# Attention gated by an FFN: the output projection in float16 pairs, and the heads of two query blocks in alternation

## Chip, cores and metric

The kernel runs on one core of a Trainium2 chip. The metric is device time in microseconds (us) of one execution; lower is better.

## What is computed

The input x is 1024 rows of 512. With xn its layer norm, the result is x + s · silu(f), where s is the attention of xn and f a gated feed-forward network of xn with weights kept as integers, scales and zeros in groups of 128. The reference, cut to the attention:

```python
q = (x @ Wq.T).reshape(b, s, H, HD).transpose(0, 2, 1, 3)      # 32 heads of 128
k = (x @ Wk.T).reshape(b, s, HKV, HD).transpose(0, 2, 1, 3)    # 8 groups
v = (x @ Wv.T).reshape(b, s, HKV, HD).transpose(0, 2, 1, 3)
q = _rmsnorm(q, q_norm_w)
k = _rmsnorm(k, k_norm_w)
scores = jnp.einsum('bkgqd,bksd->bkgqs', qg, k) / math.sqrt(HD)
bias = jnp.where(rel > 0, NEG_INF, slopes[:, :, None, None] * rel)   # causal, ALiBi
attn = jax.nn.softmax(scores + bias[None], axis=-1)
out = jnp.einsum('bkgqs,bksd->bkgqd', attn, v)
return out.transpose(...).reshape(b, s, H * HD) @ Wo.T
```

All of it is float32. The kernel gets that accuracy from pairs: a number is held as a high and a low part, and each product is three matmuls (`mm3`: high·high, high·low, low·high).

## The kernel before

The order of the work is written out by hand: each engine executes its instructions in the order in which the program issues them, and nothing is rescheduled. All DMAs go out from SP's queue, transposes and plain loads alike, in program order.

**The stages.** From 0 to about 137 us the program makes the gate and up products of the FFN, one of 14 column blocks at a time. From 137 to 217 us it runs the down projection: 14 passes (`it`), each with two halves (`tb`) of 12 matmuls of 512 columns. In each pass it loads, dequantizes (`dn_dequant`) and splits (`dn_split_w`, `dn_split_h`) what a later pass needs. The gate is put out to the tensor gd. Then come 12 projections (`Projection`): for each pair of key/value groups one of keys and values and two of queries, each with 8 tiles of 128 rows. Their normalized results go out to DRAM, transposed by DMA. The last projection's normalization (`inverse`, `newton`, `normalize`, `halves`) is put off and spread over steps of groups 1 to 4. During the last two projections the first eight attention steps are mixed in (`early`); the rest follow, from about 490 us to the end.

**The attention.** For each of 8 key/value groups there are 4 query blocks of 256 rows (`QB`); block qb sees 256·(qb+1) keys. A *unit* is one head of one block, and has two *steps* (`qt`), one for each 128 query rows. A step's *width* is its number of keys: 128 and 256 in block 0, 384 and 512 in block 1, 640 and 768 in block 2, 896 and 1024 in block 3. There are 256 steps, 32 in a group. Blocks come one after the other: 3, 2, 1, 0 in group 0, 2, 3, 0, 1 in groups 1 to 6, 2, 3, 1, 0 in group 7. In this text a block is eight steps.

In step n (`step`) the program issues, in this order:

- query, key and value loads that are due, and the scores of step n on TensorE (`scores`, L795 and on) into one of two PSUM buffers "s";
- the high part of a finished head (`heads_hi`, L864, ACT), which is done at step n − 10;
- for step n − 1 (`exponentials`): bias and minimum on VectorE (L816, "row"), exponential on ACT (L817);
- for step n − 3 (`split_hi`): the scaled float16 high part on ACT (L827), into one of five buffers p16;
- for step n − 4 (`split_lo`): the low part on VectorE (L836), and the DMA transpose of both parts to pT (L837);
- the low part of the finished head (`heads_lo`, L870), and the accumulation into y of a projection that is done (`accumulate`, L905 to L911);
- for step n − 9 (`AV_LAG`): the values matmuls of half the keys of that step's unit (`values`), with one projection triple (`out_proj`, three matmuls "op" of 512 columns) ahead of the last key tile.

A projection sums four heads (`part`) for each of two row tiles (`i`), so a block has eight triples. They start 18 steps after the block's first step, one a step. The head outputs oh, ol and Wo's parts woh, wol are float32r pairs. Wo is loaded and split 10 and 6 steps ahead of a group's first triple (`load_wo`; `split_wo`, with the low part on GpSimd, L782). oh carries the value scale rv of its group (L864).

In group 7 `gate_load` brings gd and x for a block, `gate_partial` on GpSimd turns y into y·gate + x, and `accumulate` multiplies the last projection by the gate, adds that and puts it out. The last block in the order has its projections (op_last) beside the heads themselves.

## Time and profile before

| What | Value |
|---|---|
| Time, median of 3 runs | 1081.96 us (1079.21 to 1083.37) |
| Profiled execution | 1087.19 us |
| Its span, first to last instruction | 1085.4 us |
| Mean granted TensorE clock | 0.987 |
| Stretch of groups 1 to 6 (steps 32 to 223) | 545.7 to 985.3 us |
| Group 7 and the end | 985.3 to 1085.4 us |

The profile is of one execution, some us from the median. Engines: PE is TensorE, PEld its weight loads (beside matmuls), DVE is VectorE, ACT is ScalarE, POOL is GpSimd, SP issues the DMAs. A line such as L836 is a line of the kernel before. A matmul's recorded duration includes its way through the array, so matmuls overlap in the record: what one costs in a full stream is the distance from start to start, and a busy PE need not be a full one. In the lists of waits the columns are the time in all, the number of waits and the longest. In the tables of stretches, each engine has its busy us and its number of instructions; then come the granted clock, the share of time that the DMA engines were busy, and GB/s. The DMA share reaches 1.20 in one stretch, so packets' times overlap in it, and a share of 1.0 is no proof of a full bandwidth.

### The profile page before, as it was taken

The page shows a single profiled execution, that of the slowest core. Times are in us where ns is not written, and L with a number is a line of the kernel's source. Part 1 is how long each engine was busy: PE and PEld are TensorE (multiplying, and loading weights), DVE is VectorE, ACT ScalarE, POOL GpSimd, SP SyncE. Part 2 cuts the span into 40 slices and gives each one's busy share as a digit, 9 for nine tenths or more (in the row PEclk, how much of TensorE's full clock was granted, in tenths as well). Part 3 has the DMA queues.
Part 4 walks back from the last instruction along what each step waited for, and adds up shares of the span by engine and source line. Part 5 has one row for each costly group of instructions (what it writes and reads, how often), then busy time and mean ns, then how long its engine had stood idle before and what let it go on. Part 6 is the DMA issues. An engine that isn't in the chain of part 4 may idle for free.

```text
span 1085.4 us, 18417 instructions
## 1 busy us (share of the span) xinstructions
PE 1025.6 (94%) x5912; PEld 621.8 (57%) x5912; DVE 885.4 (82%) x1738; ACT 797.9 (74%) x2144; POOL 362.7 (33%) x343
## 2 busy tenths in 40 slices
PE   7899899999999999997999999999899999999996
PEld 4444378744444444445667666667566676676674
DVE  7888997448777887787799897998897887979985
ACT  5777633568688776787788796887785887868872
POOL 1688653125545554341204104014031040043132
PEclk8999999999999999998999999999999999999999
DMA  5133255236989989999989999999998998999994
GB/s 198 32 114 119 67 141 155 74 124 152 237 206 202 237 196 270 223 205 203 221 170 213 190 216 193 196 201 189 206 191 178 213 201 184 193 224 220 237 192 117
DMA packets 445887, 198.10 MB, mean 183 GB/s; under 512 B 394402, under 2 KB 403934, under 8 KB 445790
## 3 DMA queue, kind: packets, MB, share of 16 engines
q1 hardware_dynamic: 445790, 196.93, 83.1%
q8 instruction: 46, 0.75, 0.3%
q14 instruction: 51, 0.42, 0.1%
HBM read 71.03 MB, written 29.36 MB: 92 GB/s over the span
## 4 chain that ended last, share of the span: by engine, by line
PE 57%; DVE 12%; ACT 11%; DMA 10%; issue 6%; POOL 2%; SPq 0%; DVEq 0%; ACTq 0%; POOLq 0%
DMA pT<-p 9%; PE gu_ps L255 6%; PE av L108 4%; PE s L108 4%; PE av L110 4%; PE av L109 4%; PE s L109 4%; PE s L110 4%; PE op L108 3%; PE op L110 3%; PE op L109 3%; ACT p L827 3%; PE ps_q L109 2%; PE ps_q L108 2%; PE ps_q L110 2%
## 5 line engine op out<-in xcount | busy, mean ns | idle before, releaser
L836 DVE SCALAR_TENSOR_TENSOR p<-pf,row,p 128x1024 f16<-128x1024 f32 (+7 forms) x256 | 216.4, 845 | 39.2 <-ACT p L827 36.3
L816 DVE CUSTOM_DVE_ANT_0 pf<-s,trel,cs 128x1024 f32<-128x1024 f32 (+7 forms) x256 | 207.5, 810 | 23.1 <-PE s L110 21.8
L817 ACT ACTIVATE pf<-pf,row 128x1024 f32<-128x1024 f32 (+7 forms) x256 | 197.0, 770 | 35.1 <-DVE row L816 33.5
L827 ACT ACTIVATE p<-pf,row 128x1024 f16<-128x1024 f32 (+7 forms) x256 | 196.9, 770 | 34.1 <-DMA pT<-p 30.1
L782 POOL TENSOR_TENSOR wol<-wor,woh 128x512 fp32r<-128x512 f32 x32 | 57.8, 1807 | 425.0 <-ACT woh L781 418.7
L108 PE MATMUL av<-pT,vT 128*128 128x256 f16 (+1 forms) x640 | 171.8, 268 | 25.6 <-DMA pT<-p 25.4
L109 PE MATMUL av<-pT,vT 128*128 128x256 f16 (+1 forms) x640 | 169.2, 264 | 0.0
L110 PE MATMUL av<-pT,vT 128*128 128x256 f16 (+1 forms) x640 | 169.2, 265 | 0.0
L108 PE MATMUL s<-kT,qT 128*128 128x512 f16 (+3 forms) x384 | 125.9, 328 | 3.8 <-DVE row L816 3.8
L109 PE MATMUL s<-kT,qT 128*128 128x512 f16 (+3 forms) x384 | 125.6, 327 | 0.0
L108 PEld LDWEIGHTS <-vT 128*128 128x128 f16 x640 | 62.5, 98 | 108.8 <-issue 84.6
L110 PE MATMUL s<-kT,qT 128*128 128x512 f16 (+3 forms) x384 | 123.8, 327 | 0.0
L108 PE MATMUL op<-woh,oh 128*128 128x512 f32 x248 | 121.9, 492 | 0.0
L864 ACT ACTIVATE oh<-av,rv 128x256 fp32r<-128x256 f32 x128 | 60.0, 468 | 57.5 <-PE av L110 56.3
L110 PE MATMUL op<-woh,ol 128*128 128x512 f32 x248 | 98.9, 399 | 0.0
L109 PE MATMUL ps_q<-wl_q,xth 128*128 128x512 f16 x256 | 97.7, 382 | 0.8 <-DVE wl_q L535 0.8
L108 PE MATMUL ps_q<-wh_q,xth 128*128 128x512 f16 x256 | 97.8, 382 | 0.6 <-ACT wh_q L534 0.6
L109 PE MATMUL op<-wol,oh 128*128 128x512 f32 x248 | 97.7, 394 | 0.0
L110 PE MATMUL ps_q<-wh_q,xtl 128*128 128x512 f16 x256 | 97.6, 381 | 0.0
L870 DVE SCALAR_TENSOR_TENSOR ol<-av,rv,oh 128x256 fp32r<-128x256 f32 x128 | 61.2, 478 | 21.8 <-ACT oh L864 21.7
L609 POOL TENSOR_TENSOR f_q<-f_q,inv_q 128x512 f32<-128x512 f32 x64 | 76.9, 1226 | 1.3
L109 PEld LDWEIGHTS <-vT 128*128 128x128 f16 x640 | 63.7, 99 | 11.9 <-issue 2.5
(184 smaller groups left out, 2263.5 us busy)
## 6 DMA issues: line engine op xcount, KB each, us to landing
qd<-tr_q SPq DMA_DIRECT2D x64, 256.0 KB, 3.5
qT<-qd SPq DMA_DIRECT2D x32, 512.0 KB, 4.4
wq<-in_wq SPq DMA_DIRECT2D x32, 256.0 KB, 4.1
wor<-in_wo SPq DMA_DIRECT2D x32, 256.0 KB, 3.6
gui<-in_gu_w SPq DMA_DIRECT2D x13, 512.0 KB, 3.6
wkv<-in_wkv SPq DMA_DIRECT2D x16, 256.0 KB, 3.8
vd<-v SPq DMA_DIRECT2D x8, 512.0 KB, 4.2
kd<-tr_kv SPq DMA_DIRECT2D x32, 128.0 KB, 2.5
```

What stands on the lines that cost most here:

```text
L108: te.matmul(ps, lhsT=lh, rhs=rh, start=first, stop=False)
L109: te.matmul(ps, lhsT=lh, rhs=rl, start=False, stop=False)
L110: te.matmul(ps, lhsT=ll, rhs=rh, start=False, stop=last)
L255: te.matmul(banks[j][:, k, :], lhsT=w[:, j, ws], rhs=x[:, j, k * 512 : k * 512 + 512], start=x is xth, stop=x is xtl)
L609: ge.tensor_tensor(f, f, ib, ALU.mult)
L782: ge.tensor_tensor(wol[g, i], raw, woh[g, i].bitcast(F32), ALU.subtract)
L816: ve.tensor_tensor_reduce(p, ps, trel[g][:, S - w :], cs[:, hh : hh + 1], 3e38, ALU.add, ALU.min, least[:, c])
L817: se.activation(p, p, AF.Exp, bias=least[:, c], scale=-1.0, accum_out=total[:, c])
L827: se.activation(p16[u, qt][:, :, 0, :], pf[u, qt], AF.Copy, scale=scale[:, qt : qt + 1])
L836: ve.scalar_tensor_tensor(lo, p, scale, hi, ALU.mult, ALU.subtract)
L864: se.activation(oh, av_ps[u], AF.Copy, scale=rv[:, g : g + 1])
L870: ve.scalar_tensor_tensor(ol, av_ps.pop(u), rv[:, g : g + 1], oh.bitcast(F32), ALU.mult, ALU.subtract)
```

## The change

**Format.** oh, ol, woh and wol become float16 instead of float32r. Wo is scaled by a factor for each group: the squares of each group's Wo rows are summed during the down projection (`wo_squares_load`, `wo_squares`: from pass 3 a load of 1 MB, two passes later a square of 128 x 2048 with a sum on ACT, eight of each), turned into an approximate reciprocal root for each group late in the projections (`wo_factors`, three short parts), and applied to each raw Wo tile on GpSimd (`scale_wo`, 8 steps ahead of the group's first triple). The value scale moves from oh into Wo, and `accumulate` undoes the factor with a scalar operand. There are four raw Wo buffers instead of two, and twelve oh and ol instead of eight.

**Order.** Groups 1 to 6 have two pairs of blocks, (2, 1) and (3, 0), of 16 steps each. Within a pair the heads alternate: head 0 of block 2, head 0 of block 1, head 1 of block 2, and so on. Groups 0 and 7 keep their order.

**Projections by step.** A table is made ahead (`op_at`, `acc_at`): a pair's 16 triples begin 10 steps after the pair's last step, one a step, so those of the first block of a pair start later than now by up to eight steps, as do all that queue behind them. For the last two blocks but the final one, two triples a step are allowed. Loads of queries, keys and values and the gate's loads and sums get steps of their own: queries at 6 and 10 of a pair, keys at 22 and values at 30 of a group, four query buffers instead of two; the last gate load at step 259 instead of 251, its sum at 263 instead of 259.

The diff, without unchanged lines and the five new small tiles:

```diff
-FIRST_ORDER = (3, 2, 1, 0)
-ORDER = (2, 3, 0, 1)
-LAST_ORDER = (2, 3, 1, 0)
+FIRST_ORDER = ((3,), (2,), (1,), (0,))
+ORDER = ((2, 1), (3, 0))
+LAST_ORDER = ((2,), (3,), (1,), (0,))
...
+KEYS_STEP = 22
+VALUES_STEP = 30
...
-KEYS_BLOCK = 2
-VALUES_BLOCK = 3
...
+WO_SCALE = 8
...
-GATE_LOADS = [25, 26, 28, 30]
-GATE_SUMS = [27, 28, 30, 31]
-GATE_STEP = 2
+GATE_LOADS = [211, 219, 235, 259]
+GATE_SUMS = [227, 243, 251, 263]
...
+OH_BUFS = 12
...
+    wo_raw = {}
+    def wo_squares_load(g):
+        wo_raw[g] = gp.tile([P, NH, DM], F32, tag=("gs", "us")[g % 2], name=f"wo_sq{g}")
+        sp.dma_start(wo_raw[g], wo[g * NH * HD : (g + 1) * NH * HD, :].rearrange("(i p) c -> p i c", p=P))
+    def wo_squares(g):
+        w = wo_raw.pop(g).rearrange("p i c -> p (i c)")
+        se.activation(w, w, AF.Square, accum_out=swo[:, g : g + 1])
...
-                ve.tensor_scalar(rv[:, 2 * self.i : 2 * self.i + 2], self.ri, 1.0 / (X_SCALE * P_SCALE), None, ALU.mult)
+                ve.tensor_scalar(rv[:, 2 * self.i : 2 * self.i + 2], self.ri, 1.0 / X_SCALE, None, ALU.mult)
...
         def split_head(self, i):
...
+                if 0 <= it - 3 < HKV:
+                    wo_squares_load(it - 3)
+                if 0 <= it - 5 < HKV:
+                    wo_squares(it - 5)
...
-    blocks = [(g, qb) for g in range(HKV) for qb in (FIRST_ORDER if g == 0 else ORDER if g < HKV - 1 else LAST_ORDER)]
-    units = [(g, qb, hh) for g, qb in blocks for hh in range(NH)]
+    blocks = [(g, qbs) for g in range(HKV) for qbs in (FIRST_ORDER if g == 0 else ORDER if g < HKV - 1 else LAST_ORDER)]
+    units = [(g, qb, hh) for g, qbs in blocks for hh in range(NH) for qb in qbs]
...
     def load_queries(g, qb):
-        qT[g, qb] = ap1.tile([P, NQT, 2, NH, P], F16, tag="qT", name=f"qT{g}_{qb}")
+        qT[g, qb] = ap1.tile([P, NQT, 2, NH, P], F16, tag="qT", name=f"qT{g}_{qb}", bufs=4)
...
+    def wo_factors(k):
+        if k == 0:
+            ve.tensor_tensor(rvs, rv, rv, ALU.mult)
+            ve.tensor_tensor(swo16, rvs, swo, ALU.mult)
+        elif k == 1:
+            wo_ps.append(ps2("wo_ps")[:, 0, :HKV])
+            te.matmul(wo_ps[0], lhsT=ones_bf, rhs=swo16, start=True, stop=True)
+        else:
+            ve.tensor_scalar(sg, wo_ps.pop(), 1.0 / W_SCALE**2, 1e-30, ALU.mult, ALU.max)
+            rsqrt_seed(sg, sg)
+            ve.reciprocal(isg, sg)
+            ve.tensor_tensor(rvs, rv, sg, ALU.mult)
     def load_wo(g, i):
-        wor[g, i] = late[0].tile([P, DM], F32, tag="wor", name=f"wor{g}_{i}", bufs=2)
+        wor[g, i] = late[0].tile([P, DM], F32, tag="wor", name=f"wor{g}_{i}", bufs=4)
...
+    def scale_wo(g, i):
+        ge.tensor_scalar(wor[g, i], wor[g, i], rvs[:, g : g + 1], None, ALU.mult)
     def split_wo(g, i):
-        woh[g, i] = late[0].tile([P, DM], F32R, tag="woh", name=f"woh{g}_{i}", bufs=5)
-        wol[g, i] = late[0].tile([P, DM], F32R, tag="wol", name=f"wol{g}_{i}", bufs=5)
+        woh[g, i] = late[0].tile([P, DM], F16, tag="woh", name=f"woh{g}_{i}", bufs=5)
+        wol[g, i] = late[0].tile([P, DM], F16, tag="wol", name=f"wol{g}_{i}", bufs=5)
...
-        ge.tensor_tensor(wol[g, i], raw, woh[g, i].bitcast(F32), ALU.subtract)
+        ge.tensor_tensor(wol[g, i], raw, woh[g, i], ALU.subtract)
...
     def relative(g):
...
     def heads_hi(u):
-        oh = late[0].tile([P, QB], F32R, tag="oh", name=f"oh{u}", bufs=8)
-        ol = late[0].tile([P, QB], F32R, tag="ol", name=f"ol{u}", bufs=8)
-        g = units[u][0]
-        se.activation(oh, av_ps[u], AF.Copy, scale=rv[:, g : g + 1])
-        oT[u] = (oh, ol)
+        oh = late[0].tile([P, QB], F16, tag="oh", name=f"oh{u}", bufs=OH_BUFS)
+        ol = late[0].tile([P, QB], F16, tag="ol", name=f"ol{u}", bufs=OH_BUFS)
+        se.activation(oh, av_ps[u], AF.Copy, scale=1.0 / P_SCALE)
+        oT[units[u]] = (oh, ol)
...
     def heads_lo(u):
-        oh, ol = oT[u]
-        g = units[u][0]
-        ve.scalar_tensor_tensor(ol, av_ps.pop(u), rv[:, g : g + 1], oh.bitcast(F32), ALU.mult, ALU.subtract)
-    nb = len(units) // NH
-    def out_proj(b, i, part):
+        oh, ol = oT[units[u]]
+        ve.scalar_tensor_tensor(ol, av_ps.pop(u), 1.0 / P_SCALE, oh, ALU.mult, ALU.subtract)
+    final = blocks[-1][0], blocks[-1][1][0]
+    def out_proj(g, qb, i, part):
...
-            op_ps[b, i] = last_ps[i] if b == nb - 1 else ps1("m", f"op{b}_{i}")
-        oh, ol = oT[b * NH + part]
-        g = blocks[b][0]
+            op_ps[g, qb, i] = last_ps[i] if (g, qb) == final else ps1("m", f"op{g}_{qb}_{i}")
+        oh, ol = oT[g, qb, part]
...
-        mm3(op_ps[b, i], (oh[:, cols], ol[:, cols]), (woh[g, part], wol[g, part]), part == 0, part == NH - 1)
+        mm3(op_ps[g, qb, i], (oh[:, cols], ol[:, cols]), (woh[g, part], wol[g, part]), part == 0, part == NH - 1)
...
-    def gate_load(b):
-        g, qb = blocks[b]
+    def gate_load(qb):
...
-        gates[b] = gx
-    def gate_partial(b, i):
-        g, qb = blocks[b]
-        gx, yt = gates[b], y_[0][:, qb * NQT + i, :]
+        gates[qb] = gx
+    def gate_partial(qb, i):
+        gx, yt = gates[qb], y_[0][:, qb * NQT + i, :]
...
-    def accumulate(b, i):
-        g, qb = blocks[b]
-        ps = op_ps.pop((b, i))
+    def accumulate(g, qb, i, other=False):
+        ps = op_ps.pop((g, qb, i))
...
+        undo = isg[:, g : g + 1]
...
-            ve.tensor_copy(yt, ps)
+            ve.tensor_scalar(yt, ps, undo, None, ALU.mult)
...
-            ve.tensor_tensor(yt, yt, ps, ALU.add)
+            ve.scalar_tensor_tensor(yt, ps, undo, yt, ALU.mult, ALU.add)
...
-            gt = gates[b][:, 0, i]
-            ve.tensor_tensor(gt, gt, ps, ALU.mult)
-            (ge if (b, i) == (nb - 2, NQT - 1) else ve).tensor_tensor(gt, gt, yt, ALU.add)
+            gt = gates[qb][:, 0, i]
+            ve.scalar_tensor_tensor(gt, ps, undo, gt, ALU.mult, ALU.mult)
+            (ge if other else ve).tensor_tensor(gt, gt, yt, ALU.add)
...
+    op_at, acc_at, q_at, op_first = {}, {}, {}, {}
+    begin, free = 0, 0
+    for k, (g, qbs) in enumerate(blocks[:-1]):
+        steps = BS * len(qbs)
+        for qb, lead in zip(blocks[k + 1][1], (6, 10) if steps > BS else (2, 5)):
+            q_at.setdefault(begin + lead, []).append((blocks[k + 1][0], qb))
+        begin += steps
+        due = begin + AV_LAG + 1
+        n, taken = max(free, due), 0
+        op_first.setdefault(g, n)
+        for qb in qbs:
+            for i in range(NQT):
+                for part in range(NH):
+                    op_at.setdefault(n, []).append((g, qb, i, part))
+                    if part == NH - 1:
+                        acc_at.setdefault(n + 1, []).append((g, qb, i))
+                    taken += 1
+                    if taken == 2 or n < due + NH or k < len(blocks) - 3:
+                        n, taken = n + 1, 0
+        free = n + (taken > 0)
...
-            b = u // NH
-            if qt == 0 and hh == 1 and b + 1 < nb:
-                load_queries(*blocks[b + 1])
-            if qt == 0 and hh == 3 and g + 1 < HKV:
-                if b % NB == KEYS_BLOCK:
+            for due in q_at.get(n, ()):
+                load_queries(*due)
+            if g + 1 < HKV:
+                if n % (NB * BS) == KEYS_STEP:
...
-                elif b % NB == VALUES_BLOCK:
+                elif n % (NB * BS) == VALUES_STEP:
...
-        b, r = divmod(n - AV_LAG - BS - 2, BS)
-        if 0 <= b < nb - 1 and r % NH == NH - 1 and n < nn + AV_LAG + 1:
-            accumulate(b, r // NH)
+        if n < nn + AV_LAG + 1:
+            for due in acc_at.get(n, ()):
+                accumulate(*due)
...
-        m = n - AV_LAG - BS - 1
...
         def project():
-            b, r = divmod(m, BS)
-            if 0 <= b < nb - 1:
-                out_proj(b, *divmod(r, NH))
+            for due in op_at.get(n, ()):
+                out_proj(*due)
...
-        if done is not None and done // NH == nb - 1:
-            if done % NH == 0:
+        if done is not None and units[done][:2] == final:
+            g, qb, hh = units[done]
+            if hh == 0:
...
-                out_proj(nb - 1, i, done % NH)
-            if done % NH == NH - 1:
-                accumulate(nb - 2, NQT - 1)
+                out_proj(g, qb, i, hh)
+            if hh == NH - 1:
+                for due in acc_at.get(nn + AV_LAG + 1, ()):
+                    accumulate(*due, other=True)
...
-                    accumulate(nb - 1, i)
-        b, r = divmod(n - AV_LAG, BS)
-        if r == 2 and b in GATE_LOADS:
-            gate_load(nb - NB + GATE_LOADS.index(b))
-        if b in GATE_SUMS and 0 <= r - GATE_STEP < NQT:
-            gate_partial(nb - NB + GATE_SUMS.index(b), r - GATE_STEP)
-        for lead, act in ((WO_SPLIT, split_wo), (WO_LOAD, load_wo)):
-            w, r = divmod(m + lead, NB * BS)
-            if 0 <= w < HKV and r in range(0, 2 * NH, 2):
-                act(w, r // 2)
-    last_ps = None
+                    accumulate(g, qb, i)
+        if n in GATE_LOADS:
+            gate_load(LAST_ORDER[GATE_LOADS.index(n)][0])
+        for i in range(NQT):
+            if n - i in GATE_SUMS:
+                gate_partial(LAST_ORDER[GATE_SUMS.index(n - i)][0], i)
+        for lead, act in ((WO_SPLIT, split_wo), (WO_SCALE, scale_wo), (WO_LOAD, load_wo)):
+            for g, first in op_first.items():
+                if n + lead - first in range(0, 2 * NH, 2):
+                    act(g, (n + lead - first) // 2)
+    last_ps, wo_ps = None, []
...
+    last_kv = len(projections) - 3
+    WO_FACTORS = [(last_kv, 5), (last_kv, 7), (last_kv + 1, 0)]
...
-            load_queries(*blocks[0])
+            for qb in blocks[0][1]:
+                load_queries(0, qb)
...
+            if (k, t) in WO_FACTORS:
+                wo_factors(WO_FACTORS.index((k, t)))
...
```

## Prediction

> **What bounds the kernel now.** I read the engines' shares first, then TensorE's own waits, then the stretches of one middle group, then single instructions.
>
> ```profile
> PE 1025.6 (94%) x5912; PEld 621.8 (57%) x5912; DVE 885.4 (82%) x1738; ACT 797.9 (74%) x2144; POOL 362.7 (33%) x343
> ```
> ```profile
> PE av L108 <- DMA pT<-p: 25.4, 23, 2.7
> PE s L108 <- DVE row L816: 3.8, 4, 1.8
> ```
> TensorE (PE) is the bound, and its one large wait is for the transposes of the softmax tiles (pT) ahead of the values matmuls (av). The next view has group 5's four blocks of eight steps, query blocks 2, 3, 0, 1; each begins at a block's first scores matmul in the timeline.
>
> ```profile
> 840.60:859.80 19.20, 17.47 (x120) 11.27 (x119) 16.79 (x36) 15.55 (x33) 0.00 (x0) 1.00 1.11 209
> 859.80:882.10 22.30, 22.30 (x144) 14.21 (x142) 21.10 (x36) 19.58 (x35) 3.90 (x2) 1.00 1.03 207
> 882.10:900.90 18.80, 17.37 (x144) 13.65 (x142) 12.98 (x35) 13.81 (x38) 6.97 (x3) 1.00 0.99 191
> 900.90:914.10 13.20, 13.20 (x84) 8.81 (x82) 10.94 (x31) 10.08 (x29) 0.00 (x0) 1.00 0.80 160
> ```
> Columns: length, then busy PE, weight loads, DVE, ACT, POOL. Block 3 runs PE and DVE (21.10) full; in block 0 DVE has 12.98 of 18.80 to do and PE still loses time. SP's queue shows why, in group 4 (805.0 is the start of its block 0, 826.8 of block 1):
>
> ```profile
> 805.02 10.54 SPq L837 DMA_TRANSPOSE pT<-p  x3
> 815.67 0.53 SPq L769 DMA_DIRECT2D qT<-qd  x1
> 816.30 8.29 SPq L837 DMA_TRANSPOSE pT<-p  x4
> ```
> A wide transpose holds SP about 3 us (issue of width 1024: median 3.01; of 128 to 512: 1.2 to 1.4), so block 3's spill into block 0, and the narrow ones queue behind them.
>
> What a matmul costs comes from start to start, since recorded durations overlap:
>
> ```profile
> 703.05 0.27 PE L110 MATMUL av<-pT,vT 128*128 128x256 f16 x1
> 703.08 0.48 PE L108 MATMUL op<-woh,oh 128*128 128x512 f32 x1
> 703.39 0.40 PE L109 MATMUL op<-wol,oh 128*128 128x512 f32 x1
> 703.63 0.40 PE L110 MATMUL op<-woh,ol 128*128 128x512 f32 x1
> 703.87 0.28 PE L108 MATMUL av<-pT,vT 128*128 128x256 f16 x1
> ...
> 704.21 0.38 PE L108 MATMUL s<-kT,qT 128*128 128x512 f16 x1
> 704.42 0.38 PE L109 MATMUL s<-kT,qT 128*128 128x512 f16 x1
> 704.64 0.38 PE L110 MATMUL s<-kT,qT 128*128 128x512 f16 x1
> ```
> A float16 matmul of 512 columns takes 0.216 us, 0.422 ns a column. The three float32r ones end 0.71 after the av before them (703.32 to 704.03) where float16 would need 0.65, and the av behind them is late by 0.01.
>
> **What the Trainium skill says.** "TensorE: Matmul & The Clock Gate", section Weight-path perf modes: the fast weight load is on for 128 weights unless the input is FP32. The trace agrees: a load of oh takes 0.19 us, of vT or qT 0.098. Same page, Part 1: after an idle window of about 3.4 us the array runs at half clock. Here shorter waits do it: after the 2.58 us wait that ends at 673.6 the granted clock is
>
> ```profile
> 674.40:677.80 3.40, 3.40 (x14) 2.03 (x12) 0.00 (x0) 0.48 (x2) 0.00 (x0) 0.50 0.76 201
> ```
> so a wait above 2 us costs some 1.7 more. "SBUF — State Buffer", section SBUF: two separate sides: VectorE with two SBUF inputs and a GpSimd operation exclude each other. The trace agrees for the low split: at width 128 it takes 0.34, beside a POOL operation 0.98:
>
> ```profile
> 1055.36 0.34 DVE L836 SCALAR_TENSOR_TENSOR p<-pf,row,p 128x128 f16<-128x128 f32 x1
> 1065.11 0.98 DVE L836 SCALAR_TENSOR_TENSOR p<-pf,row,p 128x128 f16<-128x128 f32 x1
> ```
>
> **The change, part by part,** against the profiled span, 1085.4 us (1087.2 with what lies around it; the median of the three runs is 1082.0, 5 below).
>
> 1. *float16 pairs.* 0.71 + 0.01 − 0.65 is 0.07 in this triple; over all triples I take 0.065. With 256 triples, 16.6 us where PE is the bound. The share of each stretch stands below.
>
> 2. *Alternating heads, groups 1 to 6.* PE's columns in a group: scores 4 heads × 4608 × 3, values the same, projection 32 × 3 × 512; 159,744 × 0.422 ns = 67.4 us. Groups 2 to 6 took 75.2, 73.2, 76.8, 73.5, 71.2: mean 74.0. Of the excess of 6.6, 32 × 0.065 = 2.1 is float32r and 4.5 waits with their half clock. Now four steps hold one wide and one narrow head: (896, 1024, 128, 256) or (640, 768, 384, 512), 2304 columns in both. PE's steps of the first kind are 1.94, 3.24, 1.94, 1.30 us (scores + trailing values + one triple), 8.4 together. SP needs 1.6 + 3.0 + 1.2 + 1.2 = 7.0 of these, so nothing spills. Is a wide head's transpose in time? Count from the start of PE's first step of the wide head that follows. DVE then waits for its 896 scores (1.14), takes their minimum (1.15) and splits the 1024 tile of the head before (1.28): 3.6 us. The values of that head begin in PE five steps on, after that step's scores: 1.94 + 3.24 + 1.94 + 1.30 + 1.94 + 1.30 = 11.7. That leaves 8.1 us for issue and landing, which took 5.07 (median of width 1024, from the issue's start). The key and query loads (0.5 us each, once 2.0 for kT) are issued at steps of narrow scores; they fit in SP's 1.4 spare us. What is late next is DVE: 61.8 busy in a group without finishing work (group 5), 64 to 68 in groups 2 to 4, where the last projection's normalization falls in. That is 92 to 100% of 67.4, and block 3 shows DVE at 95% with PE full. I take 68.9 a group: 67.4, 0.3 that block 3 shows without a wait, 1.2 for DVE. 5 × (74.0 − 68.9) = 25.5. A pair's 16 triples start after both heads' blocks, eight steps later than now, so group 1 runs eight steps without projections (24 triples left, PE about 58 us) and DVE sets it: 62.5 busy at the 95% of block 3 is 65.8, against 69.7: 3.9.
>
> 3. *Group 0:* 14 triples before its end: 0.9.
>
> 4. *Group 7 and the tail* (100.1 now). The eight late triples arrive here, 8 × 0.65 = 5.2, and the values trailing in from group 6 are wider (9 steps × 128 columns × 3 × 0.422 ns = 1.5). Against that 50 triples × 0.065 = 3.3, and 6.2 us of waits now, of which I leave 2, since the late triples fill them: 0.8 gained. The last gate load moves from step 251 to 259, where it waits for the output of block 2 that frees its buffer; nothing is behind it on SP but outputs. Load 5, then POOL 2 × 2.8, about 11 us, beside some 15 us of PE work: hidden; if not, up to 3.
>
> 5. *Sums of Wo's squares* in the down projection: eight loads of 1 MB and eight squares of 128x2048. From ACT at L817 (394 ns at 128, 1147 at 1024) a square is about 2.0 + 0.2 us. ACT is busy 4.1 to 4.8 of 11 us there (two passes), so two squares of 2.2 fit; behind one the hh cast waits, which has 5.4 us to spare. The loads go in SP's order among the dn loads; at some 200 GB/s each takes 5 us. The first two go to free buffers, the third waits for the last gate product on POOL, with the next dn loads behind it. A dnz issued at 166.8 lands 170.1 and is used 172.3, with two passes until PE sees it. Between 0 and +8 (1 us each); I take 0.5.
>
> 6. *Small operations.* Accumulation as scalar_tensor_tensor: 742 (L204) for 680, + 0.06 × 8 = 0.5 a group on DVE; ol in float16: 421 (L568) for 478, − 0.9 a group; rv's scale leaves ACT. POOL scales Wo: half of 2970 (L792) = 1.5 us, four a group; beside a low split it can cost DVE 0 to 0.6 each, + 0.5 taken, 2.4 at most. Together nothing while PE leads. The DVE factors and their one matmul are below 1 us.
>
> Sum: 25.5 + 3.9 + 0.9 + 0.8 − 0.5 = 30.6: span 1054.8, and from the median 1082.0 − 30.6 = 1051.
>
> **Rivals.** *DVE becomes the bound:* with normalization and POOL's lock it has 65.5 to do, and gaps between engines hold it at 92%: 71 a group, 5 × 3.0 + 2 + 1 = 18: 1064. For: group 3 kept it 67.8 us busy. Against: group 6 ran at 71.2 with waits of its own. *Only the format pays:* the waits move to other heads; 16.6 less the 6.7 of late work in the tail, 10: 1072. For: DMA's share is near 1.0 in every block. Against: 2304 columns in 8.4 us are 140 GB/s, block 3 moved 207. *Slower:* a wide head's transpose misses its 8.1 us. There are 24 such heads in groups 1 to 6; the slowest landing was 7.34, and an issue of 896 ahead of it holds SP 2.1 (mean), so a miss can be 1.3 and, with half clock after a third of them, 24 × 1.3 + 8 × 1.7 = 45, less 30.6: 1096. Without the clock it decides from 1.3 us a head. *No effect* is excluded for the format by the weight load's record.
>
> **Chances.** Forecast 0.64 (own range 1043 to 1058), DVE 0.18, format only 0.10, slower 0.04, the rest for squares that delay the first stage. Range 1041 to 1070. A measurement tells 0.5% from no change, 5.4 us: faster (below 1076.5) 0.92, same 0.04, slower 0.04.
>
> **What would show it.** oh loads near 0.10 us and op starts 0.216 apart; groups of 68 to 70 us; waits of av on pT under 8 us in all; DVE above 90% in groups 1 to 4; the stretch 137 to 217 unchanged. I am wrong if av still waits for pT once per wide head, or if PE waits for the minima (row) instead.

## The result and the profile after

The changed kernel takes 1078.0 us (median of 13 runs, 1075.1 to 1080.7), against 1083.4 for the kernel before, timed alternately on the same chip (13 runs). The ratio is 0.9954, with a 95% interval from 0.9938 to 0.9970. The forecast was 1051, a gain of 30.6; some 5 us came. The profiled span went from 1085.4 to 1076.8 us; the profiled execution of the kernel before is 4 us above that kernel's median.

The first view after is the engines' shares, the second TensorE's waits (us in all, times, longest).

```profile
PE 1009.3 (94%) x5913; PEld 587.6 (55%) x5913; DVE 888.9 (83%) x1745; ACT 798.2 (74%) x2160; POOL 396.2 (37%) x375
```
```profile
PE av L111 <- DMA pT<-p: 20.9, 18, 2.8
PE s L111 <- DVE row L856: 13.8, 16, 2.5
```

PE is busy 16.3 us less, near the 16.6 that the format promised. Part of that agreement is luck: the same 5913 matmuls were busy for 1001.9 us (ls) to 1011.1 us (p_lean) in the runs below. The waits for transposes fell only from 25.4 to 20.9, where under 8 was forecast, and a second wait has grown from 3.8 to 13.8: the scores wait for a PSUM buffer that VectorE's minimum (row) reads. Of the two signs named for a wrong forecast the second is there, and the first in part: in groups 2 to 6 PE waits for pT 12 times, for 20 wide heads. The next view gives the second half of group 4's pair (3, 0) and then the four half-pairs of group 5, eight steps each: length; busy PE, weight loads, DVE, ACT, POOL; clock, DMA share, GB/s.

```profile
813.80:833.80 20.00, 18.05 (x126) 11.35 (x125) 17.35 (x38) 16.06 (x40) 7.05 (x6) 1.00 1.10 221
833.80:853.80 20.00, 17.23 (x122) 10.82 (x120) 15.84 (x36) 14.09 (x33) 0.00 (x0) 1.00 1.05 188
853.80:870.40 16.60, 16.60 (x119) 10.68 (x118) 15.05 (x36) 14.21 (x33) 0.00 (x0) 1.00 1.13 222
870.40:887.40 17.00, 17.00 (x123) 11.04 (x122) 15.60 (x31) 13.60 (x31) 7.44 (x4) 1.00 0.87 173
887.40:905.60 18.20, 17.60 (x125) 11.35 (x123) 15.92 (x34) 14.50 (x35) 7.09 (x6) 1.00 1.14 220
```

Two of these run PE full, as alternation was to have it. The loss sits in the second half of pair (3, 0) and in the half behind it. What SP's queue does around that border, in group 4:

```profile
814.96 1.17 SPq L877 DMA_TRANSPOSE pT<-p  x1
816.17 1.57 SPq L646 DMA_TRANSPOSE tr_q<-q  x1
817.83 0.52 SPq L812 DMA_DIRECT2D wor<-in_wo  x1
818.46 5.92 SPq L877 DMA_TRANSPOSE pT<-p  x3
824.43 1.04 SPq L792 DMA_DIRECT2D qT<-qd  x1
825.58 1.17 SPq L877 DMA_TRANSPOSE pT<-p  x1
826.84 0.53 SPq L651 DMA_DIRECT2D qd<-tr_q  x1
827.42 1.50 SPq L646 DMA_TRANSPOSE tr_q<-q  x1
829.01 7.01 SPq L877 DMA_TRANSPOSE pT<-p  x3
```

SP never pauses here: inside the merged rows too, it is free for 0.11 us at most between two issues. Between the transposes of the probabilities stand those of the last projection's finished tiles (L646) and their stores (L651), beside the loads. What that costs shows on the last wide tile of the group. Its low split ends at 838.2, SP comes to its transpose 3.9 us later, and TensorE waits for it in the next half:

```profile
836.96 1.29 DVE L876 SCALAR_TENSOR_TENSOR p<-pf,row,p 128x1024 f16<-128x1024 f32 x1
```
```profile
842.16 2.89 SPq L877 DMA_TRANSPOSE pT<-p  x1
```
```profile
847.96 0.27 PE L111 MATMUL av<-pT,vT 128*128 128x256 f16 x1 [1.06 <-DMA pT<-p]
```

Over all 32 transposes of this half in groups 1 to 4, a tile whose low split was done waited 3.6 us on average until SP issued its transpose. From the issue to the landing took another 4.0 us (mean of the 18 for which the trace tells it). Finally the matmuls, start to start:

```profile
718.93 0.38 PE L111 MATMUL op<-woh,oh 128*128 128x512 f16 x1
719.15 0.38 PE L112 MATMUL op<-wol,oh 128*128 128x512 f16 x1
719.36 0.38 PE L113 MATMUL op<-woh,ol 128*128 128x512 f16 x1
719.58 0.27 PE L111 MATMUL av<-pT,vT 128*128 128x256 f16 x1
```

A triple now takes 0.65 us (718.93 to 719.58), the format's price to the hundredth.

Where the time went, in stretches of the profiled executions of these two kernels and of the main experiments (us; a group begins at its first scores; "g7" is group 7 with the end):

| kernel | up to g0 | g0 | g1 | g2 to 4 | g5, 6 | g7 |
|---|---|---|---|---|---|---|
| before | 434.3 | 111.4 | 69.7 | 225.2 | 144.7 | 100.1 |
| after | 441.2 | 106.2 | 66.5 | 219.9 | 142.8 | 100.1 |
| c_format | 438.8 | 106.2 | 68.9 | 215.6 | 141.9 | 96.0 |
| l_loop | 439.0 | 105.1 | 66.6 | 217.0 | 137.6 | 105.7 |
| d_finish | 438.9 | 121.2 | 64.9 | 208.8 | 139.8 | 101.8 |
| dl | 437.9 | 121.1 | 63.7 | 204.8 | 136.4 | 102.8 |
| late_only | 441.6 | 104.7 | 66.5 | 213.7 | 140.2 | 103.2 |
| p_late | 438.5 | 106.8 | 66.3 | 210.7 | 136.8 | 102.6 |

The forecast for groups 2 to 6 was 344.5 (5 × 68.9); after took 362.7. That is the term that failed: of the 22 us by which the profiled gain (8.6) misses the forecast, 18 are there, 2 lie ahead of group 1, and 0.7 and 0.8 in groups 1 and 7. The first two columns trade: the first eight attention steps are mixed into the last projections, and the sum of the two differs by up to 5 us between kernels that are alike up to there (l_loop 544.1, p_both 549.4). One execution is behind each row, so a few us of it can be its own; that of late_only was the slowest of its six, that of p_late the fastest. Verdicts below are by the timed ratios to the kernel before, each with its 95% interval.

### The profile page after: what moved, and what is told of

It reads as the page before. It is cut to its first block, busy times and chain, and to the rows that moved or that the text cites. A ratio compares the mean times of both kernels' runs of the same rounds, so it can differ in the third digit from the quotient of the medians.

```text
span 1076.8 us, 18432 instructions
## 1 busy us (share of the span) xinstructions
PE 1009.3 (94%) x5913; PEld 587.6 (55%) x5913; DVE 888.9 (83%) x1745; ACT 798.2 (74%) x2160; POOL 396.2 (37%) x375
## 4 chain that ended last, share of the span: by engine, by line
PE 51%; DVE 16%; ACT 11%; issue 9%; DMA 8%; POOL 3%; SPq 1%; DVEq 0%; ACTq 0%; POOLq 0%
PE gu_ps L264 6%; DMA pT<-p 5%; PE av L111 3%; PE av L113 3%; PE av L112 3%; PE op L111 3%; PE op L112 3%; PE op L113 3%; DVE pf L856 3%; PE s L111 3%; PE s L112 3%; PE s L113 3%; PE ps_q L111 2%; PE ps_q L113 2%; PE ps_q L112 2%
## 5 line engine op out<-in xcount | busy, mean ns | idle before, releaser
L876 DVE SCALAR_TENSOR_TENSOR p<-pf,row,p 128x640 f16<-128x640 f32 (+7 forms) x256 | 222.8, 870 | 37.4 <-ACT p L867 36.7
L857 ACT ACTIVATE pf<-pf,row 128x640 f32<-128x640 f32 (+7 forms) x256 | 196.9, 769 | 64.0 <-DVE row L856 62.5
L856 DVE CUSTOM_DVE_ANT_0 pf<-s,trel,cs 128x640 f32<-128x640 f32 (+7 forms) x256 | 207.0, 809 | 4.0 <-PE s L113 2.8
L867 ACT ACTIVATE p<-pf,row 128x640 f16<-128x640 f32 (+7 forms) x256 | 196.5, 768 | 7.4 <-DMA pT<-p 3.1
L111 PE MATMUL av<-pT,vT 128*128 128x256 f16 (+1 forms) x640 | 168.5, 263 | 20.9 <-DMA pT<-p 20.9
L815 POOL TENSOR_SCALAR wor<-wor,rvs 128x512 f32<-128x512 f32 x32 | 57.2, 1788 | 275.3 <-DMA wor<-in_wo 273.0
L111 PE MATMUL s<-kT,qT 128*128 128x512 f16 (+3 forms) x384 | 126.0, 328 | 14.1 <-DVE row L856 13.8
L112 PE MATMUL op<-wol,oh 128*128 128x512 f16 x248 | 94.2, 380 | 0.0
L111 PE MATMUL op<-woh,oh 128*128 128x512 f16 x248 | 94.2, 380 | 0.0
L113 PE MATMUL op<-woh,ol 128*128 128x512 f16 x248 | 94.2, 380 | 0.0
L903 ACT ACTIVATE oh<-av 128x256 f16<-128x256 f32 x128 | 48.0, 375 | 46.5 <-PE av L113 46.0
L908 DVE SCALAR_TENSOR_TENSOR ol<-av,oh 128x256 f16<-128x256 f32 x128 | 53.6, 418 | 29.8 <-ACT oh L903 29.3
```

Of the source, the lines that this page charges most:

```text
L111: te.matmul(ps, lhsT=lh, rhs=rh, start=first, stop=False)
L112: te.matmul(ps, lhsT=lh, rhs=rl, start=False, stop=False)
L113: te.matmul(ps, lhsT=ll, rhs=rh, start=False, stop=last)
L815: ge.tensor_scalar(wor[g, i], wor[g, i], rvs[:, g : g + 1], None, ALU.mult)
L856: ve.tensor_tensor_reduce(p, ps, trel[g][:, S - w :], cs[:, hh : hh + 1], 3e38, ALU.add, ALU.min, least[:, c])
L857: se.activation(p, p, AF.Exp, bias=least[:, c], scale=-1.0, accum_out=total[:, c])
```

## The experiments

### Which half of the change earns, and which costs

c_format: the changed kernel without the alternation.

```diff
-ORDER = ((2, 1), (3, 0))
+ORDER = ((2,), (3,), (0,), (1,))
```

> The changed kernel with one edit: groups 1 to 6 take their query blocks one after the other again (2, 3, 0, 1), so that float16 pairs, squares and scaling stay and the alternation goes. If the format alone earns what the prediction gave it (256 triples x 0.065 us, less some 1 for the squares) and the alternation costs the rest: 1066 to 1070. If the waits for transposes swallow the format's gain, as they do wherever PE isn't the bound: 1076 to 1080.

Measured: 1069.2 us, ratio 0.9882 (0.9866 to 0.9897). The format alone is worth 12 us, and alternation with its later projections costs 8 to 9 of them. The table says where: groups 2 to 6 are 5.2 longer in after, and group 7, where the late triples arrive, is 4.1 longer; group 1, which runs eight steps without triples, is only 2.4 shorter for that.

### First guesses that missed

a_loads: the loads of keys, values and Wo move from pair (3, 0) to pair (2, 1); the next group's bias is prepared where it was, and group 0's Wo is loaded where it was.

```diff
-KEYS_STEP = 22
-VALUES_STEP = 30
+KEYS_STEP = 6
+VALUES_STEP = 14
...
-WO_LOAD = 10
+WO_LOAD = 24
...
```

> The changed kernel with the loads of the next group's keys (step 6 instead of 22), values (14 instead of 30) and of Wo (24 steps ahead instead of 10) moved out of the pair (3, 0) into the pair (2, 1); POOL's work stays where it is. Theory DMA: pair (3, 0) has 3 MB of loads beside 4.7 MB of transposes in 34 us, 227 GB/s[...], so wide transposes land late; with the loads moved, groups 2 to 6 fall from 72.5 us to about 69.5, the time to 1060 to 1066. Theory POOL: nothing moves, 1076 to 1080.

Measured: 1080.2, ratio 0.9991 (0.9980 to 1.0003); the waits for pT were 22.1 us, those for the row 13.8, and the time is some 4 us above after. That doesn't clear the loads. In groups 1 to 4 a tile's wait for SP fell from 3.6 us to 2.1 in the second half of pair (3, 0), but rose from 1.5 and 0.5 to 3.8 and 2.3 in the two halves of pair (2, 1), where the loads went; in groups 1 to 6 PE's waits for pT in the second of these halves went from none to 8.8 us. The queue's delay moved with the loads.

b_noscale: GpSimd's scaling of Wo is left out.

```diff
-        ge.tensor_scalar(wor[g, i], wor[g, i], rvs[:, g : g + 1], None, ALU.mult)
+        pass
```

> The changed kernel without the scaling of Wo on POOL (left out: Wo goes unscaled into its float16 parts, so the output isn't the reference's). 32 operations of 1.8 us leave POOL in the pairs (3, 0). Theory POOL: they [...]make the low splits late, and with them the minima and transposes; groups 2 to 6 fall to 70, the time to 1062 to 1068. Theory DMA: at most the few low splits gain, 1074 to 1079.

Measured: 1074.8, ratio 0.9936 (0.9915 to 0.9956). The row waits fell to 9.0, those for pT rose to 25.7. The scaling is worth 2 to 3 us, not clear of noise (the intervals of this run and of after overlap), and is not the main part. GpSimd's other work beside VectorE is still there in this run.

f_factors: the factors' matmul, for which TensorE waits 4.0 us until 433, is put four tiles later.

```diff
-    WO_FACTORS = [(last_kv, 5), (last_kv, 7), (last_kv + 1, 0)]
+    WO_FACTORS = [(last_kv, 5), (last_kv + 1, 3), (last_kv + 1, 4)]
```

> The changed kernel with the factor matmul of Wo four tiles later (last-but-one projection, tile 3 instead of tile 7 of the one before), so that PE doesn't wait for VectorE there (4.1 us, followed by 6.8 us at half clock). If that loss reaches the end: 1070 to 1073. If the start of the attention hides it (step 16 began only 1.0 us later than before): 1075 to 1079.

Measured: 1078.5, ratio 0.9974 (0.9963 to 0.9985), no better than after. Group 0 begins 6.9 us earlier than in after, but ends at 547.8, where after ends it at 547.4: the wait and the slow clock behind it are made up by then.

h_tail: the catching up of late triples begins two entries of the list of blocks earlier, with the triples of group 6's last pair.

```diff
-                    if taken == 2 or n < due + NH or k < len(blocks) - 3:
+                    if taken == 2 or n < due + NH or k < len(blocks) - 5:
```

> The changed kernel, with the projections' triples placed two a step from the last pair of group 6 on, as the kernel in order has them for its last three blocks, instead of from the second block of group 7. If the 4.2 us by which group 7 and the tail are longer than with the format alone is the late triples that are left for it, group 7 falls by 3 to 4 us and the time is 1073 to 1076. If it is something else (the wider last values, VectorE's backlog from group 6), 1077 to 1080.

Measured: 1082.8, ratio 1.0023 (1.0012 to 1.0035), slower than before and outside both expectations; group 7 grew from 100.1 to 108.8 us. Triples brought forward overtake Wo:

```profile
PE op L112 <- POOL wol L822: 2.8, 1, 2.8
```

A wait that after does not have, with new waits for the row at three steps of group 7 beside it (2.4 us). Hurrying the late triples in this way costs more than it saves.

### The two theories: a ring of two engines, and finishing work

The timelines of ACT and DVE in after's group 5 suggested a ring: the row minimum, its exponential, the high split behind that on ACT, the low split behind that on DVE, and the next minimum behind that.

```profile
895.25 1.15 ACT L857 ACTIVATE pf<-pf,row 128x1024 f32<-128x1024 f32 x1 [1.80 <-DVE row L856]
```
```profile
893.94 1.27 DVE L856 CUSTOM_DVE_ANT_0 pf<-s,trel,cs 128x1024 f32<-128x1024 f32 x1
...
896.92 0.48 DVE L876 SCALAR_TENSOR_TENSOR p<-pf,row,p 128x256 f16<-128x256 f32 x1 [0.23 <-ACT p L867]
...
899.26 1.15 DVE L876 SCALAR_TENSOR_TENSOR p<-pf,row,p 128x896 f16<-128x896 f32 x1 [0.73 <-ACT p L867]
...
902.99 1.27 DVE L856 CUSTOM_DVE_ANT_0 pf<-s,trel,cs 128x1024 f32<-128x1024 f32 x1
```

Each engine waits for the other, and both idle. The minima of width 1024 are 9.05 us apart, though PE's four steps need 8.43 (19,968 columns at the 0.422 ns of the prediction).

l_loop: on ACT the high split of the older tile goes ahead of the newest exponential (the minimum stays where it was).

```diff
...
-        for stage, lag in ((exponentials, 1), (split_hi, NQT + 1), (split_lo, NQT + 2)):
+        for stage, lag in ((exponentials, 1), (split_hi, NQT + 1), (exponent, 1), (split_lo, NQT + 2)):
```

> The changed kernel, with ScalarE's step written in another order: the high split of the older tile stands ahead of the exponential of the newest, which waits for VectorE's row minimum. Theory 'loop': in the second half of pair (3, 0) the minimum, its exponential, the high split behind that exponential and the low split behind that high split form a ring over two engines that each work in order, and four steps of it take 9.05 us where the matmuls need 8.43. With the order turned the high split no longer waits for the newest minimum and the ring is open: the waits of the scores for the row fall from 13.8 us to under 5, the middle groups fall from 72.5 to about 70.5 and the time is 1066 to 1072. Rival 'slack': VectorE itself is full there, since no narrow block follows in which it catches up; then the order on ScalarE is worth nothing: 1075 to 1080, waits for the row above 10 us.

Measured: 1075.2, ratio 0.9946 (0.9930 to 0.9962); the row waits 10.0. By its time this can't be told from after. By the profile the ring was there and is open, for the same minima now stand 8.43 apart, PE's own pace:

```profile
885.17 1.28 DVE L856 CUSTOM_DVE_ANT_0 pf<-s,trel,cs 128x1024 f32<-128x1024 f32 x1
...
893.60 1.27 DVE L856 CUSTOM_DVE_ANT_0 pf<-s,trel,cs 128x1024 f32<-128x1024 f32 x1
```

Group 5 has three such turns. The first went from 9.82 to 8.70 and the third from 9.05 to 8.43, but the second stayed (9.91 and 9.86). It is 9.86 in dl below too, where PE never waits in this pair, so one long turn alone is no proof of a ring; that the turn answers to the order on ACT is. Groups 5 and 6, without finishing work, came down to 68.8 each, the forecast. Groups 2 to 4 came down by only 1 each, and group 7 gave 5.6 back: its first block waits 3.2 us for pT where after waits 1.1, its third 2.1 for 1.2, and in this execution each of the two waits was followed by 3.4 us at half clock, in after neither.

d_finish: the last projection is finished at once, in group 0, not over groups 1 to 4.

```diff
-            c = TILES - early + BS * (NB * (1 + t // 2) + FINISH_BLOCK) + 4 * (t % 2) if last else clock[0] + i
+            c = clock[0] + i
```

> The changed kernel, with the finishing of the last projection not spread over groups 1 to 4 but done at once, in group 0. Rival 'slack': it is this work (and GpSimd's part in it) that no longer fits beside two alternating heads; groups 2 to 4 fall from 73.3 to group 6's 71.0 and the waits for the row from 13.8 us to under 6, for which group 0 pays up to 5 us: 1070 to 1077. Theory 'loop': the ring does not need this work; groups 2 to 4 stay above 72.5 and the row waits above 9 us: 1077 to 1083.

Measured: 1079.2, ratio 0.9981 (0.9968 to 0.9993). The time lies where the loop theory had it and misses this rival's, but for another reason: groups 2 to 4 did what the rival said and more, they fell to 69.6 each, and group 0 paid 15 us for it where up to 5 were taken.

dl: both.

> Both at once: the last projection's finishing done in group 0, and the high split ahead of the exponential on ScalarE. If the finishing in groups 2 to 4 and the ring over two engines are all of what the middle groups lack to the 68.9 that was forecast, groups 2 to 6 take 68.3 to 69.0 each (342 to 345 us in all, against 362.7), while group 0 keeps its 15 us more: 1068 to 1073. If a third cause is left (loads, transposes), a group stays above 69.5 and the sum above 348.

Measured: 1068.1, ratio 0.9874 (0.9856 to 0.9893). Groups 2 to 6 take 341.2 us, 68.2 each. Group 5 and the half before it, as above:

```profile
810.20:827.50 17.30, 17.30 (x126) 11.30 (x124) 16.08 (x35) 14.65 (x35) 8.01 (x6) 1.00 1.05 223
827.50:844.40 16.90, 16.90 (x122) 10.95 (x120) 15.45 (x36) 13.84 (x34) 0.00 (x0) 1.00 0.98 185
844.40:861.00 16.60, 16.60 (x119) 10.68 (x118) 15.33 (x37) 14.03 (x33) 0.00 (x0) 1.00 1.11 218
861.00:878.00 17.00, 17.00 (x123) 11.03 (x122) 15.31 (x33) 14.57 (x34) 7.82 (x4) 1.00 0.93 182
878.00:895.20 17.20, 17.20 (x125) 11.23 (x123) 15.82 (x35) 14.55 (x35) 7.94 (x6) 1.00 1.09 225
```

PE is busy in every microsecond of these, with DVE at 90 to 93% and the DMA engines carrying as much as in after. Only 0.8 a group is left over the columns' 67.4, so the ring and the finishing are nearly all of it, and without finishing work neither VectorE nor the DMA engines bound an alternating group. In time the ring is worth 11 us here (d_finish 0.9981, dl 0.9874), while opening it in after gave nothing; the record doesn't show why.

### Which part of the finishing costs

A tile of finishing is a normalization on GpSimd, a copy and a subtraction on VectorE (0.42 and 0.69 us, medians), and on SP a transpose of 1024 columns and a store (1.3 to 2.0 and 0.5 to 1.1 us; 1.5 and 0.5 in group 4). First VectorE.

m_engine (on after) and lm (on l_loop): copy on ACT, subtraction on GpSimd, for this projection.

```diff
-            ve.tensor_copy(hi, f)
-            ve.tensor_tensor(lo, f, hi, ALU.subtract)
+            if self.k == len(projections) - 1:
+                se.copy(hi, f)
+                ge.tensor_tensor(lo, f, hi, ALU.subtract)
...
```

> The changed kernel, with the last projection's float16 halves made on ScalarE (the high one) and GpSimd (the low one) instead of VectorE, in the same steps. With that finishing work taken out of groups 1 to 4, groups 2 to 4 fell from 73.3 to 69.6 us. If it is VectorE's 1 us a tile that does not fit, they fall to about 70.5 here too, and the time is 1068 to 1073. If it is the two transposes and two stores on SP's queue, or GpSimd's normalization beside VectorE, that are too much, they stay above 72.5: 1075 to 1081.

> The high split ahead of the exponential, and the last projection's halves made on ScalarE and GpSimd. If VectorE is what the finishing overloads: groups 2 to 4 at 69.5 to 70.5, 1064 to 1070. If SP's queue or GpSimd is: 1072 to 1077.

Measured: m_engine 1077.9, ratio 0.9968 (0.9955 to 0.9980); lm 1076.6, ratio 0.9950 (0.9931 to 0.9969). Groups 2 to 4: 218.0 and 216.9. Nothing is won. That would clear VectorE's two operations a tile if GpSimd took them over without harm, but its subtraction takes 1.28 us (m_engine) and may hold VectorE up, so the run doesn't decide.

ls (on l_loop): one tile in each half of a pair (3, 0) instead of two at the end of the second.

```diff
-FINISH_BLOCK = 3
+FINISH_BLOCK = 2
...
+ 4 * (t % 2) if last
+ BS * (t % 2) if last
```

> The high split ahead of the exponential, and the last projection's finishing spread thinner: one tile in each half of a pair (3, 0) instead of two tiles at the end of the second half. With the ring open VectorE works 15.3 of 16.9 us in the first and 15.4 to 16.1 of 17.3 in the second half of a pair without finishing; a tile costs it about 1 us and fits in each, two do not. If so, groups 2 to 4 fall from 72.3 to 69.5 to 70.5: 1064 to 1070. If a tile does not fit either, the time stays at 1072 to 1077.

Measured: 1069.4, ratio 0.9891 (0.9867 to 0.9915), as expected in time and some 6 us under l_loop, but groups 2 to 4 fell only to 214.7. VectorE's work and SP's move together here, so it doesn't say which of them gained.

p_lean (on l_loop): the normalization joined with the halves, scaled copies on ACT and scaled subtractions on VectorE, a head at a time; GpSimd has none of it.

```diff
+                for i in range(n):
+                    s = self.inv[t // HT][0][:, n * r + i : n * r + i + 1]
+                    se.activation(hi[:, i], f[:, i], AF.Copy, scale=s)
+                    ve.scalar_tensor_tensor(lo[:, i], f[:, i], s, hi[:, i], ALU.mult, ALU.subtract)
...
```

> The high split ahead of the exponential, and the last projection normalized and split in one step by ScalarE (scaled copies per head) and VectorE (scaled subtractions per head): GpSimd's normalization and VectorE's copy are gone, transposes and stores stay. If GpSimd beside VectorE is the cost, groups 2 to 4 fall to 206 to 210 us in all: 1065 to 1070. If the transposes are, they stay above 213: 1072 to 1077.

Measured: 1076.8, ratio 0.9953 (0.9941 to 0.9965), groups 2 to 4 220.9. GpSimd's normalization alone isn't it, though VectorE pays here: four subtractions of 0.38 us a tile and 1.0 of waiting for ACT, for 1.1 us before. SP is left to be tried by itself.

p_notr (on l_loop): the tiles are stored as they are.

```diff
+            if self.k == len(projections) - 1:
+                sp.dma_start(qd[self.i][t], a16.rearrange("p a g d -> p (a g d)"))
+                return
             sp.dma_start_transpose(tr, a16.rearrange("p a g d -> p (a g d)"))
...
```

> The high split ahead of the exponential, and the last projection's eight tiles stored as they are, without their DMA transpose (so the query heads of the last group are wrong in the output): the transposes of 1024 columns and the stores after them, about 3 us of SP's queue a tile, are left out of groups 1 to 4, the work of VectorE and GpSimd stays. If SP's queue, full in the second half of pair (3, 0), is what the finishing overloads, groups 2 to 4 fall from 72.3 to 68.5 to 69.5 (206 to 209 us in all against 217): 1065 to 1069. If it is VectorE or GpSimd, they stay above 213: 1072 to 1077.

p_late (on l_loop): transposes and stores 12 steps later, which in the trace puts them about the middle of the next pair (2, 1): the transposes at its steps 4 to 10, the stores at 9 to 14.

```diff
-            defer(2 if self.k == len(projections) - 1 else 1, lambda: self.transposed(t, a16))
+            defer(14 if self.k == len(projections) - 1 else 1, lambda: self.transposed(t, a16))
```

> The high split ahead of the exponential, and the last projection's transposes and stores 12 steps later, in the second half of the next pair (2, 1), where SP is busy 12 to 15 of 16.6 us instead of 16 to 20 of 18 to 20. If SP's queue is the cost and has room there, groups 2 to 4 fall to 207 to 211 us in all: 1065 to 1070. If it is VectorE or GpSimd: 1072 to 1077. If SP has no room there either, the second half of pair (2, 1) grows beyond 16.6.

Measured: p_notr 1065.3, ratio 0.9856 (0.9832 to 0.9879); p_late 1067.5, ratio 0.9870 (0.9844 to 0.9896). Groups 2 to 4: 211.4 and 210.7, each some 6 of the 12 us between l_loop (217.0) and dl (204.8). Having the transposes somewhere else is worth as much as not having them. The sum for groups 2 to 4 is 2 us above the range expected of p_notr and inside that of p_late. The other half of the cost is elsewhere.

What may be that half shows in l_loop's group 3, on VectorE, and beside it on GpSimd:

```profile
737.76 1.38 DVE L640 CAST q<-f_q 128x512 f16<-128x512 f32 x1
739.17 1.06 DVE L641 TENSOR_TENSOR q<-f_q,q 128x512 f16<-128x512 f32 x1
...
741.30 2.23 DVE L881 SCALAR_TENSOR_TENSOR p<-pf,row,p 128x1024 f16<-128x1024 f32 x1
...
743.80 1.27 DVE L856 CUSTOM_DVE_ANT_0 pf<-s,trel,cs 128x1024 f32<-128x1024 f32 x1
```
```profile
736.86 2.00 POOL L822 TENSOR_TENSOR wol<-wor,woh 128x512 f16<-128x512 f32 x1
...
741.30 1.16 POOL L822 TENSOR_TENSOR wol<-wor,woh 128x512 f16<-128x512 f32 x1 [0.73 <-ACT woh L821]
```

Copy, subtraction and the wide low split take 1.38, 1.06 and 2.23 us beside GpSimd's Wo work, where 0.42, 0.69 and 1.27 are usual: 2.3 us late together, and the scores of step 123 wait 1.6 us for that last minimum, until 745.1. In p_late such waits are what is left in groups 2 to 6 (5.5 us for the row, 0.6 for pT). For the subtraction and the low split, which read two tensors in SBUF, this fits the Trainium skill, "SBUF — State Buffer", section SBUF: two separate sides: of such a VectorE operation and a GpSimd operation, the one that starts first holds a shared port for its whole instruction and blocks the other. The trace agrees: the low split ends 1.07 us after the GpSimd operation beside which it began (742.46), and the next GpSimd operation, begun inside the low split, took 2.32 us for the usual 1.57. How much of the half this overlap makes up was not taken apart; m_engine, which moves work from VectorE to GpSimd, may have failed for the same reason.

### The repair by itself, and the best versions

late_only: the changed kernel with p_late's line alone.

> The changed kernel with nothing but the last projection's transposes and stores 12 steps later. With the ring opened first, this took 6.3 us from groups 2 to 4. If the transposes and the ring cost independently, groups 2 to 4 fall from 219.9 to about 213.5 us and groups 5 and 6 stay at 142 to 143: 1070 to 1074. If the transposes matter only once the ring is open, the time stays at 1076 to 1080; if they are the larger part without it, below 1070.

Measured: 1067.5, ratio 0.9863 (0.9836 to 0.9890), in the third range of the expectation, though groups 2 to 4 fell to 213.7 as the first had it. It is no worse than p_late: in the time the open ring adds nothing on top, in the profile 6.4 us of groups 2 to 6. SP's queue at the same border, for comparison with the second view of after:

```profile
808.34 1.17 SPq L877 DMA_TRANSPOSE pT<-p  x1
809.61 0.52 SPq L812 DMA_DIRECT2D wor<-in_wo  x1
810.22 6.43 SPq L877 DMA_TRANSPOSE pT<-p  x3
816.70 0.83 SPq L792 DMA_DIRECT2D qT<-qd  x1
817.64 8.31 SPq L877 DMA_TRANSPOSE pT<-p  x4
```

The last row's four transposes have 1.1 us of idle queue among them: SP has caught up and waits for the next tile, where in after it ran behind. The same wide tile as in after is now issued as soon as its low split is done:

```profile
830.57 1.26 DVE L876 SCALAR_TENSOR_TENSOR p<-pf,row,p 128x1024 f16<-128x1024 f32 x1
```
```profile
831.86 2.42 SPq L877 DMA_TRANSPOSE pT<-p  x1
```

Over groups 1 to 4 the wait for SP in this half fell from 3.6 to 0.8 us on average, while from issue to landing the transposes took 4.0 us as before. So it is the queue of issues that was too full there, and not the DMA engines behind it. PE's waits for pT in groups 2 to 6 fell from 12.1 to 2.9 us. One number, 14 for 2, is worth about 10 us.

c_late: the same line in c_format.

> The float16 format with the heads in order and the last projection's transposes and stores 12 steps later, which puts them beside the widest heads. If the finishing's transposes are what groups 2 to 5 have above group 6's 68.8 in this order too, they fall from 72.2 to 69 to 70: 1058 to 1064, and the alternation has earned nothing over the order. If there SP's queue is as full beside the widest heads (20 of 21.8 us), nothing is won: 1067 to 1071.

Measured: 1070.4, ratio 0.9882 (0.9855 to 0.9908), nothing won. With the heads in order the deferred transposes fall beside the widest block and the one ahead of it, and SP works 20.5 to 20.7 of the widest block's 21.8 us. The alternation does make room in SP's queue. Whether it is worth having is another question: late_only (0.9863) and c_late or c_format (0.9882 both) don't come apart by their intervals. In the profile late_only's groups 2 to 6 are 3.6 us under c_format's (p_late's 10.0), and its group 7 is 7.2 longer (6.6).

c_loop: c_format with the high split ahead.

> The float16 format without the alternation (heads of one query block at a time), with the high split ahead of the exponential on ScalarE. In order, the wide heads' values wait 22.5 us for the split probabilities; the high split standing behind the newest exponential is part of that road, so it should shorten by up to an exponential a head: 1064 to 1068 against the format's 1069 if so, 1068 to 1071 if the transpose or VectorE's low split alone sets it.

Measured: 1071.9, ratio 0.9920 (0.9905 to 0.9935), above both expectations and some 3 us above c_format. Nothing is won with the heads in order; where the 3 us go was not followed.

p_both (on ls): one tile a half, transposes in the next pair (2, 1).

```diff
-            defer(2 if self.k == len(projections) - 1 else 1, lambda: self.transposed(t, a16))
+            defer(20 - 4 * (t % 2) if self.k == len(projections) - 1 else 1, lambda: self.transposed(t, a16))
```

> The version to beat both kernels: the high split ahead of the exponential, one tile finished in each half of a pair (3, 0), and its transpose and store in the second half of the next pair (2, 1). If VectorE's 1.1 us a tile and SP's 3 us a tile both count, groups 2 to 4 come to 68.5 to 69.5: 1060 to 1066. If only one counts, 1066 to 1070.

Measured: 1065.3, ratio 0.9849 (0.9824 to 0.9873), the fastest version with the whole computation, some 17 us below before and 11 to 13 below after. By its interval it doesn't come apart from late_only and p_late, and hardly from c_format. Groups 2 to 4 came to 209.7, not below 208.5: the row waits fell to 4.6, but waits for pT returned (20.8).

## Why the prediction was wrong, step by step

1. *float16 pairs, 16.6:* right in mechanism and price, 0.65 us a triple. As a gain in time it is 12 (c_format), with the squares and the small operations in it. Why not all 16.6 arrive is not shown.

2. *Alternating heads:* the failed step. It put "I take 68.9 a group: 67.4, 0.3 that block 3 shows without a wait, 1.2 for DVE"; 72.5 was measured, 18.2 us over five groups. Two pieces of its working were wrong.
   - "SP needs 1.6 + 3.0 + 1.2 + 1.2 = 7.0 of these, so nothing spills" counts the probabilities' transposes, and beside them only key and query loads. The finished tiles of the last projection were left out: two transposes and two stores per group, 2 × (1.5 + 0.5) = 4 us of SP, beside Wo's, the keys' and the values' loads. In the text they appear as VectorE's work only. Without them SP issues for 16.0 to 16.4 of that half's 17.3 us (dl, groups 2 to 5), so 4 more don't fit. They made a finished tile wait 3.6 us for its issue (0.8 in late_only). Moved away they free 6.2 us of groups 2 to 4 and 2.6 of 5 and 6, of which group 7 takes 3.1 back in that execution (late_only), and some 10 in the time.
   - "Is a wide head's transpose in time?" gave it 8.1 us, with VectorE waiting for its scores. In that half VectorE runs behind instead. For a wide tile at the end of group 5, counted as the prediction counts, from PE's first step of the next wide head (896.6), the low split ended 6.1 us in and not 3.6, and the values were wanted at 11.7 as forecast. The transpose landed 0.3 us before that: 5.5 us of room, all used.
   - What was taken as "1.2 for DVE" holds two things that a busy share doesn't show: a ring through ACT, 9.05 us for 8.43 (1.7 to 2.6 a group in groups 5 and 6, of which group 7 gives a part or all back), and what finishing costs beside SP, some 6 us over groups 2 to 4. GpSimd's stretch of VectorE's operations is seen in it, its share is not known.
   With ring and finishing away a group takes 68.2 (dl), 0.7 under the forecast. So the columns and the 2304 per four steps were right, and DVE and the DMAs suffice for a group without finishing; with it, as in groups 2 to 4, that was not shown.

   Group 1 was right, in mechanism too: 66.5 for the 65.8 forecast, with 5.0 us of waits for the row and none for pT.

3. *Group 0, 0.9:* groups and lead-in trade too much between executions to tell.

4. *Group 7 and the tail, 0.8 gained:* 0.0 measured. PE's waits there fell from 5.8 to 2.7 us, where 6.2 to 2 was taken, which is the 0.8. Against c_format, which has no late triples, it is 4.1 worse.

5. *Sums of Wo's squares, −0.5:* from its first matmul to its last the down projection takes 79.0 us for 77.6 before, −1.4 and inside its range.

6. *Small operations "together nothing":* the prices held (accumulation 743 ns, ol 418), but POOL ahead of a 1024-column low split costs VectorE 0.4 to 0.9 us in after, where 0 to 0.6 was taken. "The DVE factors and their one matmul are below 1 us" was a wait of 4.0, hidden as f_factors shows.

The prediction's "a wait above 2 us costs some 1.7 more" held for the 2.58 us that it read, and is no rule. The wait for the row of 2.54 us late in group 2 was followed by half clock in late_only (667.6 to 671.0) and not in after.

The rival *DVE becomes the bound* was near in group time (71). For groups without finishing dl refutes it; in groups 2 to 4 some 6 us of finishing may still lie on VectorE and GpSimd, as it said. *Only the format pays* at 1072 was nearest in time, and what it expected, waits that move to other heads, is seen: 12.1 us for pT in groups 2 to 6, for 13.3 before. What stays open: why group 7, with the heads alternating, takes 1 to 6 us more where groups 5 and 6 take less (in l_loop longer waits and two stretches at half clock account for it, which may be chance), why the ring counts in the time only with the finishing gone, how much of the finishing's second half is GpSimd's overlap and how much the place of VectorE's work, and whether alternation, so mended, beats the format alone.

## What to carry to other kernels

When work is moved to a new order, list what else is already pinned to fixed steps there, and price each of its instructions on every queue, SP's too: two transposes and two stores a group cost some 10 of the 30 us forecast, and 12 steps of delay brought them back. A queue that is counted 83% full (7.0 of 8.4) had no room for what was not counted; find the stretch in which it never pauses, and take the time from a tile's last operation to its issue. When loads are moved out of such a stretch, look at where they land: in a_loads the delay went with them. And an engine's share says nothing about a ring: compare the distances of the same instruction over several turns with the pace of the engine that should lead, and see whether they answer to the order.
